# Start-up work moved between engines and rows, and the DMA queue in program order, in a fused window-attention and Fourier kernel

## The chip, the cores and the metric

The kernel runs on one core of one Trainium2 chip. The metric is the device time of one execution in microseconds (us), as the median of several runs. A second source is one profiled execution of the same program; its times come from the hardware profiler. Engine names in the profile: PE is TensorE (PEld its weight loads), DVE is VectorE, ACT is ScalarE, POOL is GpSimd, SP is the engine whose queue issues nearly all DMAs.

## What is computed

The input `x` holds 32 images of 56 x 56 pixels with 128 channels, in float32. Two layers follow each other, each with a residual:

```python
x = x + window_attention(group_norm(x))      # 7x7 windows, shifted by 3, 4 heads of 32
x = x + fourier_block(group_norm(x))         # 32 groups in both norms

# window_attention, for each of 64 windows of 49 pixels
q, k, v = split(win @ w_qkv.T);  q = q * hd ** -0.5
a = softmax(q @ k.T + bias + mask)           # bias from rpb_table, mask for the shifted edge
out = (a @ v) @ w_proj.T + b_proj

# fourier_block: along W with w0 and along H with w1
y = dct(x)[..., :32];  y = einsum("bixy,ioy->boxy", y, w);  y = idct(y padded to 56)
h = y_along_w + y_along_h
out = relu(h @ W1 + b1) @ W2 + b2            # 128 -> 512 -> 128
```

## The kernel before

**Rows and cycles.** The work is a software pipeline. An image has eight window rows (`NWR = 8`), and the main loop runs over cycles; cycle `r` is also called row `r`, counted from 0 over all images, so that row `8 * b + i` is window row `i` of image `b`. In cycle `r` the kernel computes q, k, scores and v of row `r` (`attn_qk`, `attn_scores`, `attn_v`), the softmax of rows around it (`attn_max` with a subtraction on GpSimd, `attn_exp` on ScalarE, `attn_divide` with a multiplication on GpSimd), the transposes of the probabilities of rows `r-1` and `r-2` (`attn_transpose`), the values of row `r-3` (`attn_values`) and its projection (`attn_project`), and the sums for the second norm (`attn_sums`) of row `r-4` or near it. Rows 0 to 10 go through `first_rows`, where nothing else runs.

**The Fourier part** of an image starts 11 cycles after its first row (`CONV_BEGIN = NWR + 3`). Its step `c = r - 11 - 8 * b` runs from 0 to 15: the transforms (`transform`) along W at c = 0 and along H at 1 and 2, the mixing (`mix`) at 3, 4 and 5, the transforms back (`modes_back`) at 5 to 8, and seven groups of feed-forward (`ff_in`, `ff_out`) at the steps of `FF_AT = (8, 9, 10, 12, 13, 14, 15)`. Two images are therefore in this part at once. Feed-forward first runs in row 19; later it is missing from one row in eight, where c is 3 for one image and 11 for the other (row 22, 30 and so on). What a step passes on goes through DRAM: `scr` (the residual stream), `zscr` (mixed modes). `load_columns` reads `htok` tiles from `scr`, `load_modes` reads `zT` tiles from `zscr`, `ff_in` reads `res` from `scr`, and `ff_out` writes `out_dram` from it.

**The next image.** Its load (`xl`, two buffers) is issued by `image_begin` at window row 3 of the image before, the second part at row 4. `image_groups(im, j)` turns rows `j` and `j+1` by seven TensorE transposes into two PSUM banks, copies them to `xw` on ScalarE (three copies), takes statistics on VectorE (L297) and adds the projection's bias into the image on GpSimd (`image_bias`, L306). Four such calls make an image. `image_norm` is a Python generator: each `next(norm)` emits one stage, namely the group statistics on VectorE with the power on GpSimd (`rstd`, L355); then `nb` on VectorE (L359) and the scaling of the weights on ScalarE (`wn`, L362); then a small matmul for the bias of v (L112, `pa<-nb,wqkv`) and its copy (`bqkv`, L367). `fourier_stats` does the same for the second norm (`tot`, L581, then two matmuls with `gmean`).

**PSUM and order.** There are eight PSUM banks, four for attention (`attn_bank`, `pa` in the profile) and four for the rest (`conv_bank`, `pc`). On PE, ACT, DVE and POOL the order of instructions is the order of the program, written out by hand:

```python
with tc.manual_schedule(engines={ET.PE, ET.Activation, ET.DVE, ET.Pool}):
```

On SP, the DMA queue, the scheduler chooses the order; an instruction of a queue that waits holds all that stand behind it. `bias_and_mask(0)` and `bias_and_mask(1)` add bias and mask into the constant `bm` for inner rows and for the last row of an image, 16 adds of 49 x 98 each on VectorE (L193); the second runs in row 1.

Of the kernel before, what the change touches and what calls it, by code (L numbers as in the profile page):

```python
# [15 lines left out]
P = 128  # L16
# [32 lines left out]
def swin_fourier_kernel(  # L49
# [33 lines left out]
    def attn_bank():  # L83
        return bank("pa", 4)
# [87 lines left out]
            )  # L172
    nc.sync.dma_start(rpb[JP : JP + WT], rpb[0:WT])

    mask_sb = work.tile([P, 4, C], F32, tag="sq", name="mask", bufs=1).rearrange("p n c -> p (n c)")
    mask_sb = mask_sb[:, : 4 * WT].rearrange("p (r k j) -> p r k j", r=2, k=2)
    nc.vector.memset(mask_sb, 0.0)
    for hh in range(2):
# [5 lines left out]
    nc.gpsimd.memset(bm, 0.0)  # L184
    rpb_f = rpb.rearrange("p (t u) y x -> p t u (y x)", u=2)

    def bias_and_mask(r):
        for t in range(2):
            for half in range(2):
                rows = slice(half * JP, half * JP + WT)  # L190
                for k, p0, p1 in ((0, 0, NP - half), (1, NP - half, NP)):
                    for p in range(p0, p1):
                        nc.vector.tensor_tensor(  # L193
                            bm[rows, r, t, p],
                            rpb_f[rows, t],
                            mask_sb[rows, r, k].unsqueeze(1).to_broadcast([WT, 2, WT]),
                            ALU.add,
                        )

    bias_and_mask(0)  # L200
    dct_w = const_load([TC, 2 * NM], dct, "dct_w")
    dct_h = const.tile([TC, 2 * NM], F32, tag="dct_h", name="dct_h")
    for r in range(0, TC, S):
# [63 lines left out]
    def image_groups(im, i):  # L267


        pt = [attn_bank(), attn_bank()]  # L270
        pts = [
            p[:, : n * S].rearrange("p (j r s) -> p j r s", r=n, s=WS) for p, n in zip(pt, (8, 6))
        ]
        for c in range(7):
            nc.tensor.transpose(  # L275
                pts[c // 4][:, :, 2 * (c % 4) : 2 * (c % 4) + 2],
                im.x[:, WS * i // 2 + c],
                ident_x[:, :, SS:].rearrange("p r (j s) -> p j r s", s=WS),
            )
# [35 lines left out]
    def image_norm(im):  # L315

        GR = C // 16

        def average(out, src):
            sums = small.tile([P, GR], F32, tag="gsums", name="gsums", bufs=2)  # L320
            nc.vector.tensor_reduce(
                sums, src.rearrange("p (g c) -> p g c", c=4), axis=AX.X, op=ALU.add
            )
            nc.vector.tensor_scalar(
                out.rearrange("p (g c) -> p g c", c=4),
                sums.unsqueeze(2).to_broadcast([P, GR, 4]),
                0.25,
                None,
                ALU.mult,
            )  # L330
# [24 lines left out]
        nc.gpsimd.tensor_tensor(rstd, ve, mhalf, ALU.pow)  # L355
        im.w = work.tile([P, 3 * C], F32, tag="wn", name="wn")
        yield
        nb = small.tile([P, 1], F32, tag="nb0", name="nb0")
        nc.vector.scalar_tensor_tensor(  # L359
            out=nb, in0=gm, scalar=-1.0, in1=rstd, op0=ALU.mult, op1=ALU.mult  # L360
        )
        nc.scalar.mul(im.w, wqkv, rstd)  # L362
        yield
        pb = attn_bank()
        halved(pb[:, 0:1], wqkv[:, 2 * C :], nb)
        im.bias = small.tile([P, 5], F32, tag="bqkv", name="bqkv")
        nc.vector.tensor_copy(im.bias[:, 2:3], pb[:, 0:1])  # L367
        yield

# [365 lines left out]

    def ff_in(im, g):
        t0, n = sum(FF_GROUPS[:g]), FF_GROUPS[g]
        k, last = n // P, n % P  # L740
        xff = im.xf.rearrange("p r w -> p (r w)")
        scr_tok = im.scr.rearrange("h w c -> (h w) c")
        res = work.tile([P, 4, C], F32, tag="res", name="res")
        nc.sync.dma_start(
# [1 line left out]
        )  # L746
        if last:
            nc.sync.dma_start(res[:last, k], scr_tok[t0 + k * P : t0 + n])
        for c0, c1, m in ((0, k, P), (k, k + 1, last)):
            if m:  # L750
                nc.gpsimd.tensor_tensor(  # L751
# [83 lines left out]
    def load_back(cycle):  # L835
        for im, c in fourier(cycle):
            for width, g in back_groups(c):
                load_modes(im, width, g)

    def nothing():  # L840
        while True:
            yield

    def load_first(cycle):
        for im, c in fourier(cycle):
# [3 lines left out]

    def halves_first(cycle, norm):  # L850
        for im, c in fourier(cycle):
            if c == 0:
                im.stats = fourier_stats(im)
                im.cols = {}
                next(im.stats)
        last, j = row(cycle - 4)
        sums = attn_sums(last, j) if last and cycle > CONV_BEGIN else nothing()
        next(sums)
        im, i = row(cycle)
        if im:  # L860
            attn_qk(im, i, False)
        next(norm)
        next(sums)
        for im, c in fourier(cycle):
            if c in FF_AT:
# [25 lines left out]
                    mix(im, True, g)  # L891

    def quarters(cycle):
        im, i = row(cycle)
        if im:
            attn_scores(im, i, cycle)
        for im, c in fourier(cycle):
            for width, g in back_groups(c):
                modes_back(im, width, g)

    def eighths(cycle):
        im, i = row(cycle - 3)
# [13 lines left out]
    def next_groups(cycle):  # L916
        b, i = divmod(cycle, NWR)
        if b + 1 < NB:
            for j in {(4 if b == 0 else 5): (0, 2), (5 if b == 0 else 6): (4, 6)}.get(i, ()):
                image_groups(images[b + 1], j)  # L920

    def last_out(cycle):
# [4 lines left out]
    def halves_last(cycle, norm):  # L927
# [6 lines left out]
        load_back(cycle + 1)  # L934
        next_begin(cycle)
        load_first(cycle)
        next(norm)
        if row(cycle)[0]:
            attn_exp(cycle)
            attn_divide(cycle)  # L940
# [1 line left out]
        if im:  # L942
            last_out(cycle)
            attn_project(im, j)
        next(norm)

    def next_begin(cycle):
        b, i = divmod(cycle, NWR)
# [7 lines left out]
    def first_rows(cycle, norm):  # L956
# [15 lines left out]
            attn_max(cycle)  # L972
        if im3:
            attn_project(im3, i3)
        next(norm)
        last, j = row(cycle - 4)
        if last:
            for _ in attn_sums(last, j):
# [2 lines left out]
            attn_v(im, i, cycle)  # L981
        if cycle < NWR // 2:
            image_bias(im, 2 * cycle)
        if cycle == 1:
            bias_and_mask(1)
        next(norm)
        next_begin(cycle)
        next_groups(cycle)
        if cycle == CONV_BEGIN - 1:
            attn_exp(cycle)  # L990
            attn_divide(cycle)
            for _ in attn_sums(im3, i3):
                pass
            last, j = row(cycle - 1)
            attn_transpose(last, j, cycle - 1)
        next(norm)

    ET = mybir.EngineType
    with tc.manual_schedule(engines={ET.PE, ET.Activation, ET.DVE, ET.Pool}):
        images[0] = image_begin(0)  # L1000
        for i in range(0, NWR, 2):
            image_groups(images[0], i)
        for _ in image_norm(images[0]):
            pass
        norm = nothing()
        for cycle in range(NB * NWR + CONV_BEGIN + FF_AT[-1] - NWR + 1):
            if cycle < CONV_BEGIN:
                first_rows(cycle, norm)
            else:
# [10 lines left out]
                    half_columns(cycle)  # L1020
                eighths(cycle)
                quarters(cycle)
                if row(cycle)[0] and cycle % 2:
                    attn_max(cycle)
                full(cycle)
                halves_last(cycle, norm)
            b, i = divmod(cycle, NWR)
            norm = nothing()
            if i == (NWR - 2 if b else NWR - 3) and b + 1 < NB:
                norm = image_norm(images[b + 1])  # L1030
                next(norm)


# [60 lines left out]
```

## Time and profile before

| | |
|---|---|
| median of 3 runs | 3635.16 us (3634.94 to 3637.57) |
| profiled execution | 3641.7 us, span 3639.9 us |
| mean granted TensorE clock | 0.995 of full speed |
| busy share PE, PEld, DVE, ACT, POOL | 98%, 78%, 61%, 59%, 38% |
| DMA | 390.31 MB, mean 107 GB/s |

The span is the time from the first to the last instruction of the profiled execution. A line of the profile names the source line, the engine, the operation, the tiles (written tile before the arrow) and the shape. In a timeline the first two numbers are start and duration in us, and a bracket gives the idle time before and the event that ended it; "issue" there means that the profile shows no event. In the list of waits the three numbers are the total, the count and the longest. Much of a helper's work has the line of the helper: L112 is `halved`, which issues most matmuls.

### The profile page before, as it was taken

The page shows a single profiled execution, that of the slowest core. Times are in us where ns is not written, and L with a number is a line of the kernel's source. Part 1 is how long each engine was busy: PE and PEld are TensorE (multiplying, and loading weights), DVE is VectorE, ACT ScalarE, POOL GpSimd, SP SyncE. Part 2 cuts the span into 40 slices and gives each one's busy share as a digit, 9 for nine tenths or more (in the row PEclk, how much of TensorE's full clock was granted, in tenths as well). Part 3 has the DMA queues.
Part 4 walks back from the last instruction along what each step waited for, and adds up shares of the span by engine and source line. Part 5 has one row for each costly group of instructions (what it writes and reads, how often), then busy time and mean ns, then how long its engine had stood idle before and what let it go on. Part 6 is the DMA issues. An engine that isn't in the chain of part 4 may idle for free.

```text
span 3639.9 us, 161666 instructions
## 1 busy us (share of the span) xinstructions
PE 3574.4 (98%) x72192; PEld 2832.6 (78%) x72192; DVE 2211.9 (61%) x4738; ACT 2148.1 (59%) x4044; POOL 1368.3 (38%) x1421
## 2 busy tenths in 40 slices
PE   7899999999999999999999999999999999999999
PEld 5677777778777787877777878777777777787776
DVE  7766666666666666666656656666566666565641
ACT  4555566655566555666556665556665556655553
POOL 5433333333343433333333434333333334343321
PEclk8999999999999999999999999999999999999999
DMA  4334434444434444334444344443444443444343
GB/s 114 86 102 112 113 96 111 108 110 111 112 97 112 112 109 116 94 110 107 113 108 111 94 114 109 113 114 94 111 108 111 110 111 94 114 109 109 97 115 98
DMA packets 687350, 390.31 MB, mean 107 GB/s; under 512 B 39967, under 2 KB 657600, under 8 KB 686400
## 3 DMA queue, kind: packets, MB, share of 16 engines
q1 hardware_dynamic: 686045, 379.65, 38.3%
q8 instruction: 568, 9.31, 1.1%
q14 instruction: 126, 1.03, 0.1%
q10 hardware_dynamic: 611, 0.32, 0.0%
HBM read 218.29 MB, written 161.48 MB: 104 GB/s over the span
## 4 chain that ended last, share of the span: by engine, by line
PE 92%; DVE 4%; issue 1%; ACT 1%; POOL 1%; DMA 1%; SPq 0%; POOLq 0%; DVEq 0%; ACTq 0%
PE pc L112 37%; PE pa L112 14%; PE pa L408 6%; PE pc L679 6%; PE pa L474 6%; PE pc L645 6%; PE pa L430 5%; PE pa L499 4%; PE pc L718 4%; PE pa L275 3%; DVE a L438 1%; DVE xf L729 0%; DVE oT L530 0%; POOL rstd L616 0%; ACT a L455 0%
## 5 line engine op out<-in xcount | busy, mean ns | idle before, releaser
L449 POOL TENSOR_TENSOR a<-a,mx 128x784 f32<-128x784 f32 x256 | 389.4, 1521 | 1427.3 <-DVE mx L448 1203.4
L112 PE MATMUL pc<-wff,hid 128*64 128x128 f32 x12544 | 740.3, 273 | 1.5 <-ACT hid L763 0.8
L112 PE MATMUL pc<-xf,wff 128*64 128x512 f32 (+2 forms) x3584 | 717.5, 539 | 1.1 <-DVE xf L729 1.0
L112 PEld LDWEIGHTS pc<-wff,hid 128*64 128x64 f32 x12544 | 702.6, 137 | 8.2 <-ACT hid L763 4.5
L460 DVE TENSOR_REDUCE sm<-a 128x16 f32<-128x784 f32 x256 | 248.2, 970 | 686.1 <-ACT a L455 682.8
L463 POOL TENSOR_TENSOR a<-a,rs 128x784 f32<-128x784 f32 x256 | 389.1, 1520 | 566.6 <-DVE rs L462 542.8
L763 ACT ACTIVATE hid<-pc,b1sb 128x512 f32<-128x512 f32 (+2 forms) x896 | 527.1, 632 | 76.6 <-PE pc L112 74.5
L112 PEld LDWEIGHTS pc<-xf,wff 128*64 128x64 f32 x3584 | 279.8, 137 | 368.0 <-issue 260.5
L379 ACT ACTIVATE q<-pa,bqkv 128x392 f32<-128x392 f32 x256 | 150.4, 587 | 473.1 <-PE pa L112 467.5
L112 PE MATMUL pa<-xw,wn 128*64 128x392 f32 (+1 forms) x2048 | 390.6, 497 | 3.7 <-DVE aT L484 2.7
L530 DVE TENSOR_SCALAR oT<-pa,bqkv 128x98 f32<-128x98 f32 (+2 forms) x768 | 171.0, 278 | 268.7 <-PE pa L499 268.6
L751 POOL TENSOR_TENSOR res<-res,b2sb 128x512 f32<-128x512 f32 (+2 forms) x256 | 264.2, 1037 | 113.5 <-DMA res<-scr 113.5
L408 PE MATMUL pa<-wn,xw 128*64 128x128 f32 x4096 | 283.6, 280 | 4.7 <-issue 3.5
L306 POOL TENSOR_TENSOR xl<-xl,bproj 112x512 f32<-112x512 f32 (+1 forms) x256 | 286.8, 1142 | 0.0
L499 PEld LDWEIGHTS pa<-aT,v 49*32 49x32 f32 x16384 | 172.9, 106 | 146.1 <-issue 127.0
L415 ACT COPY v<-pa 128x512 f32<-128x512 f32 x256 | 150.9, 589 | 228.3 <-PE pa L408 228.3
L438 DVE TENSOR_TENSOR a<-pa,bm 128x392 f32<-128x392 f32 x512 | 264.8, 559 | 25.8 <-PE pa L430 2.1
L455 ACT ACTIVATE a<-a 128x784 f32<-128x784 f32 x256 | 222.3, 869 | 97.2 <-POOL a L449 96.8
L482 ACT COPY aT<-pa 113x452 f32<-113x452 f32 x256 | 139.4, 544 | 210.4 <-PE pa L474 206.6
L408 PEld LDWEIGHTS pa<-wn,xw 128*64 128x64 f32 x4096 | 221.4, 137 | 38.6 <-issue 9.1
L112 PE MATMUL pa<-wproj,oT 128*64 128x128 f32 (+1 forms) x3584 | 248.0, 274 | 1.8 <-DVE oT L530 1.8
L448 DVE TENSOR_REDUCE mx<-a 128x16 f32<-128x784 f32 x256 | 246.3, 962 | 4.3
(91 smaller groups left out, 5583.8 us busy)
## 6 DMA issues: line engine op xcount, KB each, us to landing
zscr<-z SPq DMA_DIRECT2D x512, 112.0 KB
htok<-scr SPq DMA_DIRECT2D x256, 196.0 KB
zT<-zscr SPq DMA_DIRECT2D x192, 256.0 KB
res<-scr SPq DMA_DIRECT2D x160, 256.0 KB
out_dram<-res SPq DMA_DIRECT2D x160, 256.0 KB
scr<-xl SPq DMA_DIRECT2D x128, 224.0 KB
xl<-in_x_dram SPq DMA_DIRECT2D x32, 784.0 KB
xl<-in_x_dram SPq DMA_DIRECT2D x32, 672.0 KB
```

The costliest lines, as they stand in the source:

```text
L112: nc.tensor.matmul(dst[ps], lhsT=lhsT[:, ps], rhs=rhs, start=start, stop=stop)
L306: nc.gpsimd.tensor_tensor(piece, piece, bproj.unsqueeze(1).to_broadcast([TC, e - a, C]), ALU.add)
L408: nc.tensor.matmul(pv[hs, j * C : (j + 1) * C], lhsT=im.xw[i][:, w * WT : w * WT + JP], rhs=im.w[:, 2 * C : 3 * C], start=True, stop=True,)
L438: nc.vector.tensor_tensor(a[:, 2 * hp : 2 * hp + 2, :, 0:WT].rearrange("p u w j -> p w u j"), ps[hp][:, :RT].rearrange("p (w u j) -> p w u ...
L448: nc.vector.tensor_reduce(mx, a3, axis=AX.X, op=ALU.max)
L449: nc.gpsimd.tensor_tensor(a3, a3, mx.unsqueeze(2).to_broadcast([P, 2 * NWR, WT]), ALU.subtract)
L455: nc.scalar.activation(a3, a3, AF.Exp)
L460: nc.vector.tensor_reduce(sm, a3, axis=AX.X, op=ALU.add)
L463: nc.gpsimd.tensor_tensor(a3, a3, rs.unsqueeze(2).to_broadcast([P, 2 * NWR, WT]), ALU.mult)
L499: nc.tensor.matmul(po4[u][h * HD : (h + 1) * HD, 2 * f + e], lhsT=v[ks, 2 * f + e, h * HD : (h + 1) * HD], rhs=im.aT[i][f][ks, h, e * JP : ...
L751: nc.gpsimd.tensor_tensor(res[:m, c0:c1], res[:m, c0:c1], b2sb[:m].unsqueeze(1).to_broadcast([m, c1 - c0, C]), ALU.add,)
L763: nc.scalar.activation(hf[:, :n], ph[:, :n], AF.Relu, bias=b1sb[:, f : f + 1])
```

## The change

- `image_groups` takes its two banks from the attention banks or, for every second call, from the other four. From image 2 on, all four calls stand in window row 6 of the image before; formerly two in row 5 and two in row 6. For image 1 they stay in rows 4 and 5.
- `bias_and_mask` takes an engine. The half for the last window row moves from VectorE in row 1 to GpSimd in rows 4 and 5, eight adds each. The mask is kept in a `res` buffer until then.
- The three stages of `image_norm` move apart: statistics in the same row as before, scaling in the next call, and the small matmul in the row after, behind q and k of the image's first row. For image 0 it comes after the scores of row 0.
- For image 0's second norm, `fourier_stats` starts in row 10, ahead of `attn_exp` and `attn_divide`, with `attn_sums` of row 7 ahead of them too.
- In rows without feed-forward, `modes_back` stands ahead of `attn_scores`.
- SP joins the engines in program order, and the load of `res` is issued one row earlier (`load_residual` from `load_back(cycle + 1)`).

```diff
-    mask_sb = work.tile([P, 4, C], F32, tag="sq", name="mask", bufs=1).rearrange("p n c -> p (n c)")
+    mask_sb = work.tile([P, 4, C], F32, tag="res", name="mask").rearrange("p n c -> p (n c)")
...
-    def bias_and_mask(r):
-        for t in range(2):
-            for half in range(2):
...
+    def bias_and_mask(engine, r, t, half):
+        rows = slice(half * JP, half * JP + WT)
+        for k, p0, p1 in ((0, 0, NP - half), (1, NP - half, NP)):
+            for p in range(p0, p1):
+                engine.tensor_tensor(
...
-    bias_and_mask(0)
+    for t in range(2):
+        for half in range(2):
+            bias_and_mask(nc.vector, 0, t, half)
...
-        pt = [attn_bank(), attn_bank()]
+        pt = [conv_bank() if i % 4 else attn_bank() for _ in range(2)]
...
+    def load_residual(im, g):
+        t0, n = sum(FF_GROUPS[:g]), FF_GROUPS[g]
+        k, last = n // P, n % P
+        scr_tok = im.scr.rearrange("h w c -> (h w) c")
+        res = work.tile([P, 4, C], F32, tag="res", name="res")
+        nc.sync.dma_start(
+            res[:, :k], scr_tok[t0 : t0 + k * P].rearrange("(n p) c -> p n c", p=P)
+        )
+        if last:
+            nc.sync.dma_start(res[:last, k], scr_tok[t0 + k * P : t0 + n])
+        im.next_res = res
...
     def ff_in(im, g):
-        res = work.tile([P, 4, C], F32, tag="res", name="res")
-        nc.sync.dma_start(
...
+        res = im.next_res
...
     def load_back(cycle):
...
+            if c in FF_AT:
+                load_residual(im, FF_AT.index(c))
...
+    def start_stats(im):
+        im.stats = fourier_stats(im)
+        im.cols = {}
+        next(im.stats)
...
     def halves_first(cycle, norm):
         for im, c in fourier(cycle):
-            if c == 0:
-                im.stats = fourier_stats(im)
-                im.cols = {}
-                next(im.stats)
+            if c == 0 and cycle > CONV_BEGIN:
+                start_stats(im)
...
-        next(norm)
+        if has_ff(cycle):
+            next(norm, None)
...
     def quarters(cycle):
+        def back():
+            for im, c in fourier(cycle):
+                for width, g in back_groups(c):
+                    modes_back(im, width, g)
+        if not has_ff(cycle):
+            back()
         im, i = row(cycle)
         if im:
             attn_scores(im, i, cycle)
-        for im, c in fourier(cycle):
-            for width, g in back_groups(c):
-                modes_back(im, width, g)
+        if has_ff(cycle):
+            back()
...
-            for j in {(4 if b == 0 else 5): (0, 2), (5 if b == 0 else 6): (4, 6)}.get(i, ()):
+            for j in ({4: (0, 2), 5: (4, 6)} if b == 0 else {6: (0, 2, 4, 6)}).get(i, ()):
                 image_groups(images[b + 1], j)
...
     def first_rows(cycle, norm):
...
-        if cycle == 1:
-            bias_and_mask(1)
-        next(norm)
+        if cycle in (4, 5):
+            for half in range(2):
+                bias_and_mask(nc.gpsimd, 1, cycle - 4, half)
...
         if cycle == CONV_BEGIN - 1:
+            start_stats(im3)
+            for _ in attn_sums(im3, i3):
+                pass
             attn_exp(cycle)
             attn_divide(cycle)
-            for _ in attn_sums(im3, i3):
-                pass
...
-    with tc.manual_schedule(engines={ET.PE, ET.Activation, ET.DVE, ET.Pool}):
+    with tc.manual_schedule(engines={ET.PE, ET.Activation, ET.DVE, ET.Pool, ET.SP}):
...
-        for _ in image_norm(images[0]):
-            pass
-        norm = nothing()
+        norm = image_norm(images[0])
+        for _ in range(3):
+            next(norm)
...
+                if not has_ff(cycle):
+                    next(norm, None)
                 if row(cycle)[0] and cycle % 2:
                     attn_max(cycle)
```

More of the change, by code (lines that the diff above doesn't have):

```diff
@@ L185, in swin_fourier_kernel @@
     rpb_f = rpb.rearrange("p (t u) y x -> p t u (y x)", u=2)
-    def bias_and_mask(r):
-        for t in range(2):
-            for half in range(2):
[L190 to L198, printed above, removed]
-    bias_and_mask(0)
+    def bias_and_mask(engine, r, t, half):
[3 more added lines that the diff above has]
+                engine.tensor_tensor(
+                    bm[rows, r, t, p],
+                    rpb_f[rows, t],
+                    mask_sb[rows, r, k].unsqueeze(1).to_broadcast([WT, 2, WT]),
+                    ALU.add,
+                )
+    for t in range(2):
+        for half in range(2):
+            bias_and_mask(nc.vector, 0, t, half)
     dct_w = const_load([TC, 2 * NM], dct, "dct_w")
@@ L356, in image_norm @@
         im.w = work.tile([P, 3 * C], F32, tag="wn", name="wn")
+        im.bias = small.tile([P, 5], F32, tag="bqkv", name="bqkv")
         yield
@@ L365, in image_norm @@
         halved(pb[:, 0:1], wqkv[:, 2 * C :], nb)
-        im.bias = small.tile([P, 5], F32, tag="bqkv", name="bqkv")
         nc.vector.tensor_copy(im.bias[:, 2:3], pb[:, 0:1])
@@ L734, in modes_back @@
                 nc.scalar.copy(dst[:, li], src.rearrange("p (c h r) -> p c h r", c=nch, r=2))
-    def ff_in(im, g):
+    def load_residual(im, g):
         t0, n = sum(FF_GROUPS[:g]), FF_GROUPS[g]
         k, last = n // P, n % P
-        xff = im.xf.rearrange("p r w -> p (r w)")
         scr_tok = im.scr.rearrange("h w c -> (h w) c")
@@ L748, in ff_in @@
             nc.sync.dma_start(res[:last, k], scr_tok[t0 + k * P : t0 + n])
+        im.next_res = res
+    def ff_in(im, g):
+        t0, n = sum(FF_GROUPS[:g]), FF_GROUPS[g]
+        k, last = n // P, n % P
+        xff = im.xf.rearrange("p r w -> p (r w)")
+        res = im.next_res
         for c0, c1, m in ((0, k, P), (k, k + 1, last)):
@@ L944, in halves_last @@
             attn_project(im, j)
-        next(norm)
     def next_begin(cycle):
@@ L974, in first_rows @@
             attn_project(im3, i3)
-        next(norm)
+        next(norm, None)
         last, j = row(cycle - 4)
@@ L983, in first_rows @@
             image_bias(im, 2 * cycle)
-        if cycle == 1:
-            bias_and_mask(1)
-        next(norm)
+        if cycle in (4, 5):
+            for half in range(2):
+                bias_and_mask(nc.gpsimd, 1, cycle - 4, half)
         next_begin(cycle)
@@ L989, in first_rows @@
         if cycle == CONV_BEGIN - 1:
+            start_stats(im3)
+            for _ in attn_sums(im3, i3):
+                pass
             attn_exp(cycle)
             attn_divide(cycle)
-            for _ in attn_sums(im3, i3):
-                pass
             last, j = row(cycle - 1)
             attn_transpose(last, j, cycle - 1)
-        next(norm)
     ET = mybir.EngineType
-    with tc.manual_schedule(engines={ET.PE, ET.Activation, ET.DVE, ET.Pool}):
+    with tc.manual_schedule(engines={ET.PE, ET.Activation, ET.DVE, ET.Pool, ET.SP}):
         images[0] = image_begin(0)
@@ L1022, in swin_fourier_kernel @@
                 quarters(cycle)
+                if not has_ff(cycle):
+                    next(norm, None)
                 if row(cycle)[0] and cycle % 2:
@@ L1027, in swin_fourier_kernel @@
             b, i = divmod(cycle, NWR)
-            norm = nothing()
             if i == (NWR - 2 if b else NWR - 3) and b + 1 < NB:
                 norm = image_norm(images[b + 1])
-                next(norm)
+                next(norm, None)
 def _constants():
```

## The prediction

> **What bounds the kernel now.** I read the page's shares and slices first. PE's digits, with the granted clock:
>
> ```profile
> PE 3574.4 (98%) x72192; PEld 2832.6 (78%) x72192; DVE 2211.9 (61%) x4738; ACT 2148.1 (59%) x4044; POOL 1368.3 (38%) x1421
> PE   7899999999999999999999999999999999999999
> PEclk8999999999999999999999999999999999999999
> ```
>
> TensorE is full except at the start. The windows by slice (window, PE, PEld, DVE, ACT, POOL, clock, DMA) give sizes:
>
> ```profile
> 0.00:91.00 91.00, 64.60 (x1032) 46.82 (x1032) 64.90 (x163) 44.77 (x93) 47.48 (x62) 0.89 0.45 114
> 91.00:182.00 91.00, 77.35 (x1734) 63.37 (x1732) 65.46 (x142) 53.58 (x106) 38.91 (x39) 0.94 0.32 86
> 182.00:273.00 91.00, 86.58 (x1760) 68.44 (x1762) 58.98 (x129) 51.02 (x96) 36.22 (x39) 0.98 0.37 102
> 2729.90:2820.90 91.00, 90.81 (x1850) 71.73 (x1850) 57.14 (x118) 54.34 (x102) 35.17 (x39) 1.00 0.42 111
> ```
>
> Idle: 44.5 us in the first three slices, 15 in the 36 that follow, 6 in the last. So steady rows (row = cycle, numbered from 0) can only lose, and the last slice is one image's TensorE work. All gain lies before row 19, where feed-forward fills TensorE. The waits of TensorE name what to look for, its timeline where:
>
> ```profile
> PE pa L112 <- DVE nb L359: 10.3, 3, 4.7
> PE pa L112 <- DVE tot L581: 4.0, 1, 4.0
> 77.12 0.38 PE L112 MATMUL pa<-nb,wqkv 128*64 128x1 f32 x4 [4.41 <-DVE nb L359]
> 113.39 0.34 PE L112 MATMUL pa<-tot,gmean 112*64 112x64 f32 x4 [3.97 <-DVE tot L581]
> 128.01 0.57 PE L499 MATMUL pa<-aT,v 49*32 49x49 f32 x29 [2.08 <-issue]
> ```
>
> Then the timelines of VectorE, GpSimd and the DMA queue where these idle times are:
>
> ```profile
> 33.69 6.23 DVE L193 TENSOR_TENSOR bm<-rpb,mask 49x98 f32<-49x98 f32 x16
> 40.61 0.97 DVE L460 TENSOR_REDUCE sm<-a 128x16 f32<-128x784 f32 x1
> 84.52 1.04 DVE L438 TENSOR_TENSOR a<-pa,bm 128x392 f32<-128x392 f32 x2 [0.48 <-PE pa L430]
> 56.48 1.52 POOL L449 TENSOR_TENSOR a<-a,mx 128x784 f32<-128x784 f32 x1 [0.44 <-DVE mx L448]
> 63.24 1.52 POOL L463 TENSOR_TENSOR a<-a,rs 128x784 f32<-128x784 f32 x1 [0.67 <-DVE a L438]
> 71.05 1.52 POOL L463 TENSOR_TENSOR a<-a,rs 128x784 f32<-128x784 f32 x1 [0.17 <-DVE rs L462]
> 110.39 1.78 SPq L667 DMA_DIRECT2D htok<-scr  x4
> 118.77 4.53 SPq L118 DMA_DIRECT2D xl<-in_x_dram  x5
> ```
>
> VectorE is busy 4.6 to 4.9 of every 5 us from 55 to 75; GpSimd in rows 4 and 5 waits 0.7 and 0.2 us only. Below, times are on the clock of before.
>
> **A. Mask off VectorE at row 1.** The 16 adds hold 33.69 to 39.92. The next sum (L460) starts at 40.61; without them its input binds, the exponent of row 1, 35.52 + 0.87 = 36.4 in ScalarE's timeline. Gain 4.2. The 2.68 us that TensorE idles before 40.63 go too, and with them slow matmuls (clock 0.70 and 0.62 from 40 to 50: eight transposes 1.86 us against 1.39 later): 0.8, bounds 0 and 1.6 (five slow groups). Sum -5.0 (-3.4, the sum delayed by other VectorE work, to -5.8).
>
> **B. Mask on GpSimd in rows 4 and 5, norm over three rows.** The bias matmul that waited 4.41 us moves behind row 8's q and k, nb and the weight scaling to row 7. (The first of the three nb waits, 4.7 us at 18.07 before row 0, stays for another reason: q needs the scaled weights, down at 17.77 + 0.61, and its matmul already started at 18.43. Zero.) What is late next is GpSimd. No row shows a 49x98 add on it. L751's 1277 ns for 512 columns and 730 for 256 give 2.14 ns a column, hence 392 ns at 98; bounds 185 (VectorE's first eight, 1.48 us undisturbed) and 448 (its 64x128 add). I take 392, from its own rows: eight cost 3.1 us. GpSimd then runs: subtraction of row 4 to 58.0, mask 61.1, image adds (57.94 to 62.57 before, 4.6) 65.7, multiply 67.2, subtraction of row 5 68.7, mask 71.8, adds 76.4, multiply 77.9, subtraction of row 6 79.4. Row 6's transposes (68.10) and exponent (68.67) are still met; row 7's transposes wait 2.7 us. Exponent 0.87, sum 0.97 and reciprocal 0.25 put row 7's scores add at 81.5 instead of 84.52: -3.0. The step to row 8's took 7.5 us with half-rate matmuls, the next 6.7: -0.8. Sum -3.8; with 185 ns VectorE's own queue binds at 79.6, -5.7; with 448, -2.0 without the second part.
>
> The same adds took 6.23 / 16 = 0.39 us on VectorE beside a busy GpSimd, so the move costs nothing in length. [...]
>
> An idle time near 2.7 us remains. In this trace 2.08 us was followed by clocks of 0.73 and 0.58, 2.68 us by 0.70 and 0.62, 1.79 us by 1.00; I therefore count no clock recovery there beyond the 0.8. [...]
>
> **C. Statistics ahead of the exponent, row 10.** L581 now follows row 7's residual add: mx ends 107.12, two sums 108.6, tot 109.2, two sums of row 7 110.4; matmuls at 110.5, not 113.39, -3.0. The 112 transforms behind ran 4.96 us where later ones take 3.45. VectorE's scores add of row 11 follows at 116.1, not 120.31; ScalarE's exponent at 119.9, not 124.08. Sum -4.2 (-3.0 where only the idle time goes, -5.5 where all 3.97 of it and 1.5 of slow transforms go).
>
> **D. SP in program order.** In row 11 the four column loads (htok, 196 KB each) now stand behind the first piece of image 2's load (784 KB), which waits for the last transform of image 0 at T = 118.63, since it takes its buffer. The tail shows the rate: 256 KB issued at 3615.37 let GpSimd start at 3618.19, 768 KB issued from 3587.66 at 3592.39, so 1.9 us per further 512 KB. Columns land at T + 6.4 and T + 7.8; wanted T + 4.5. Transforms end at T + 8.7, not T + 6.2, but before lost 0.37 + 2.08 just behind and ran slow: scores ended at T + 11.4, now T + 10.4. Sum -1.0 (-2.5 if the load is quicker, +3 if the 2.08 us, whose releaser is not shown, comes again on top). Later images have 13 us between transform and columns for 6.3 us of transfer: zero. Each row's zT loads now wait for the z copies (378.59 + 0.58, row 23), with 1.2 MB queued: down by about 385, wanted 388.91; zero, cover 4 us.
>
> **E. Transposes in one block.** Row 14 (image 2) has four groups. ScalarE copies a group in 0.9 us, TensorE transposes one in 0.8 to 0.95: from the aT copy's end near 151.5 the twelve copies take 3.7, then v to 155.8, z to 156.7 and 157.6 at TensorE's pace, and only then the exponent, before at 156.28. GpSimd's 9.4 us of adds end by 162.5, its multiply by 164.0, before row 15's subtraction is due (166.10). +1.2 (0 to +2.5). From image 3 on (row 22 and every eighth) no feed-forward stands in this row. Covers: the third group's banks are free at 365.18 (VectorE's second aT copy), wanted 365.7; GpSimd ends its adds at 375.7 and the multiply at 377.2, while the norm's rstd is due at 377.3. Zero; its price if cover fails is a rival.
>
> **F. Transforms back ahead of scores.** It applies only without feed-forward: rows 16, 17, 18. Scores waited for k on VectorE (0.39, 1.90, 1.70 us); the work now stands in these waits. Row 16: values end 171.05, transforms 172.9, scores 173.8, a 174.8, aT copy 175.4, where mx starts, not 175.78; row 17: VectorE binds, 0; row 18: the four xf adds (1.75) move ahead of a, mx at 195.5, not 196.56. Sum -1.4 (+1.5 if the adds wait, -2).
>
> **G. Residual a row ahead**: GpSimd's 113.5 us of waiting for it are off the chain: zero. Its issue (0.38 us on SP) moves past out_dram and scr and, in an image's row 3, past the image and column loads; none of those is late by that. The mask's other buffer and bqkv's earlier tile: zero.
>
> Sum: -5.0 - 3.8 - 4.2 - 1.0 + 1.2 - 1.4 = -14.2. The profiled execution, 3641.7 (span 3639.9 and 1.8 around it), becomes 3627.5; it lies 6.5 above the median 3635.16, which becomes **3621.0**. Ends: -21.5 all good, -1.1 all bad.
>
> **Rivals.** *Block stalls in every image*: if the four groups' copies, image adds or the SP order hold TensorE in the FF-free row, it costs 30 times. Slower by 0.2% (7.3 us, about what a measurement can tell) needs (14.2 + 7.3) / 30 = 0.72 us each; 1.65 us, the two added groups unhidden, gives 3621 + 50 = 3671. For it: the 0.5 us cover of the banks; against: 15 us idle in 36 slices says these rows have had no queue trouble. 0.11.
> *Eaten start*: GpSimd's mask at VectorE's worst (four in 3.07 us) and the column stall in full: -14.2 + 3.8 + 4 = -6.4, 3629. For it: GpSimd's short waits in rows 4 and 5. 0.14.
> *Clock*: mean clocks 0.89, 0.94, 0.98 hold 17 us over three slices; with the gaps shorter, more than I count comes back, -20 or more, 3614. 0.09.
>
> **Numbers.** Forecast case (gain 7.3 to 20) 0.66. Faster 0.75 with the clock case, same 0.14, slower 0.11. Range 3614 to 3631: below lies part of the clock case, above the stall and half of the eaten start.
>
> **What would show it.** Right: no L193 on VectorE after 26 us, none of the nb or tot waits; row 7's transposes wait about 3 us for GpSimd's multiply; a wait for htok near 115; slices 4 to 39 idle as before. Wrong: new idle of TensorE every 112 us in the row with 28 transposes; waits for zT or htok past 220 us; first-three-slice idle still above 38 us.

## The result and the profile after

| | before | after |
|---|---|---|
| median | 3636.36 us (3634.94 to 3638.27, 4 runs) | 3615.95 us (3613.83 to 3618.46, 4 runs) |
| profiled execution | 3641.7 us, span 3639.9 | 3618.46 us, span 3616.7 |

The ratio is 0.9944, 95% interval 0.9927 to 0.9961: 20.4 us faster, where 14.2 was forecast and 3614 to 3631 was the range. The time is inside the range; most of the reasons were not. Where the time went shows in a ledger: the interval between the first scores matmul of one row and that of a later row (the starts of L430, in after L431, read from the trace). Like every ledger below, it is of the one profiled execution of each kernel.

| rows | before | after | difference | forecast |
|---|---|---|---|---|
| 0 to 28 (all the start-up) | 310.1 us | 307.5 us | -2.5 | -14.2 |
| 28 to 255 (steady) | 3153.3 us | 3131.5 us | -21.8 | 0 |

Ahead of row 0 after is 0.4 us longer and behind row 255 0.8 us, so the two spans differ by 23.2 us.

The page of after looks like that of before; TensorE does the same 72192 matmuls in 17 us less busy time:

```profile
PE 3557.3 (98%) x72192; PEld 2829.6 (78%) x72192; DVE 2254.9 (62%) x4722; ACT 2145.9 (59%) x4044; POOL 1376.0 (38%) x1437
PE   7899999999999999999999999999999999999999
```

The windows by slice (columns as in the prediction) say the same from the other side: the first three slices idle 26.3, 12.5 and 3.9 us, 42.7 together where before had 44.5. The prediction had named more than 38 there as a sign that it was wrong. The 36 slices behind them idle 9.8 us where before had 14.9.

```profile
0.00:91.00 91.00, 64.69 (x1054) 47.02 (x1056) 64.60 (x146) 45.32 (x94) 52.84 (x78) 0.89 0.42 108
91.00:182.00 91.00, 78.51 (x1788) 63.71 (x1782) 65.43 (x143) 53.69 (x106) 39.19 (x39) 0.94 0.35 88
182.00:273.00 91.00, 87.08 (x1714) 67.80 (x1708) 59.84 (x127) 51.88 (x99) 36.38 (x38) 0.98 0.43 106
```

In TensorE's list of waits nb (10.3 us) and tot (4.0 us) are gone, and three others stand there (total, count, longest; the 5.1 of wn is the start of row 0, its other 3.3 is in row 16):

```profile
PE pa L112 <- ACT wn L364: 8.3, 2, 5.1
...
PE pa L475 <- POOL a L464: 3.4, 1, 3.4
PE pc L646 <- DMA htok<-scr: 3.4, 2, 3.0
```

**The steady gain is in the transposes of the next image.** TensorE's timeline in before, one steady image: two blocks of 14, each from its first start to the start of what follows 1.65 and 1.91 us, 3.56 in all:

```profile
681.28 1.72 PE L275 MATMUL pa<-ident_x,xl 112*128 112x112 f32 x14
682.93 1.09 PE L408 MATMUL pa<-wn,xw 128*64 128x128 f32 x16
...
696.06 1.98 PE L275 MATMUL pa<-ident_x,xl 112*128 112x112 f32 x14
697.97 1.09 PE L408 MATMUL pa<-wn,xw 128*64 128x128 f32 x16
```

In after the 28 stand in one block, 691.88 to 694.86, 2.98 us:

```profile
691.88 0.92 PE L276 MATMUL pa<-ident_x,xl 112*128 112x112 f32 x7
692.64 0.88 PE L276 MATMUL pc<-ident_x,xl 112*128 112x112 f32 x7
693.35 0.88 PE L276 MATMUL pa<-ident_x,xl 112*128 112x112 f32 x7
694.06 0.87 PE L276 MATMUL pc<-ident_x,xl 112*128 112x112 f32 x7
694.86 1.09 PE L409 MATMUL pa<-wn,xw 128*64 128x128 f32 x16
```

Over images 4 to 29 the means are 3.56 and 2.99. Idle time makes only 0.04 us of the difference. One transpose is recorded with 262 ns while the next starts 100 ns after it, so a wait of up to some 160 ns lies inside the recorded duration and is counted as busy. The starts of the single records tell: a step is 0.1016 us on average, 28 make 2.84; the first step of a block takes 0.05 more and the last 0.09 more (0.145 a block); and in the second block of before the 11th step takes 0.30 and the one behind it 0.157. TensorE goes on at 697.52, just when VectorE ends a copy that frees a bank:

```profile
696.85 0.62 DVE L484 COPY aT<-pa 113x452 f32<-113x452 f32 x1
```

So before pays two block entries (0.29) and 0.43 of waits for banks, after one entry (0.145) and none. 0.576 us for each of the 28 images turned between rows 28 and 255 is 16.1 of the 21.8 us. Of the other 5.7 some 4 are TensorE's idle time outside these blocks, 13.1 us in before's execution and 9.1 in after's, most of it in waits for which the profile shows no event; the remaining 1.6 us are spread over many groups, and their cause is open. Idle time between rows 28 and 255 varies between executions (7.3 to 14.2 us in all the profiles here, before's is the longest), and before's profiled execution is 5.3 us above its median where after's is 2.5 above its own.

**The start-up** gained in three places and gave most of it back. VectorE's and GpSimd's timelines in row 6 of after:

```profile
73.33 3.48 DVE L325 TENSOR_SCALAR gmeans<-gsums 128x32 f32<-128x32 f32 x1
76.84 1.45 DVE L340 TENSOR_TENSOR turned<-turned,gmeans 128x32 f32<-128x32 f32 x1
...
81.51 0.96 DVE L461 TENSOR_REDUCE sm<-a 128x16 f32<-128x784 f32 x1
...
82.74 0.97 DVE L439 TENSOR_TENSOR a<-pa,bm 128x392 f32<-128x392 f32 x2
```

```profile
73.08 2.21 POOL L307 TENSOR_TENSOR xl<-xl,bproj 112x512 f32<-112x512 f32 x2
75.25 1.52 POOL L464 TENSOR_TENSOR a<-a,rs 128x784 f32<-128x784 f32 x1
76.72 1.52 POOL L450 TENSOR_TENSOR a<-a,mx 128x784 f32<-128x784 f32 x1
```

The same two operations in before's row 6:

```profile
74.24 0.25 DVE L324 TENSOR_SCALAR gmeans<-gsums 128x32 f32<-128x32 f32 x1
74.53 0.19 DVE L339 TENSOR_TENSOR turned<-turned,gmeans 128x32 f32<-128x32 f32 x1
```

Operations that take 0.18 and 0.19 us where GpSimd rests took 3.48 and 1.45, and each ended 0.04 to 0.05 us behind a GpSimd operation (76.81 and 76.77; 78.29 and 78.24). So VectorE was late for the sum of row 7 (L461): its input, the exponent, was ready at 79.14 in ScalarE's timeline, and it began at 81.51, 2.4 us later; the scores add of row 7 (L439) stands right behind it. TensorE's timeline has what followed, with the columns and row 16's scaled weights:

```profile
76.82 1.86 PE L475 MATMUL pa<-ident,a 113*113 113x113 f32 x8 [3.41 <-POOL a L464]
...
122.95 1.04 PE L646 MATMUL pc<-dct_h,htok 112*64 112x64 f32 x28 [3.05 <-DMA htok<-scr]
...
164.72 2.64 PE L112 MATMUL pa<-xw,wn 128*64 128x393 f32 x8 [3.26 <-ACT wn L364]
```

### The profile page after: what moved, and what is told of

Read it like the earlier page. It is cut to its first block, busy times and chain, and to the rows that moved or that the text cites. A ratio compares the mean times of both kernels' runs of the same rounds, so it can differ in the third digit from the quotient of the medians.

```text
span 3616.7 us, 161664 instructions
## 1 busy us (share of the span) xinstructions
PE 3557.3 (98%) x72192; PEld 2829.6 (78%) x72192; DVE 2254.9 (62%) x4722; ACT 2145.9 (59%) x4044; POOL 1376.0 (38%) x1437
## 4 chain that ended last, share of the span: by engine, by line
PE 93%; DVE 4%; ACT 1%; POOL 1%; DMA 1%; issue 1%; SPq 0%; POOLq 0%; DVEq 0%; ACTq 0%
PE pc L112 38%; PE pa L112 15%; PE pa L409 6%; PE pc L680 6%; PE pa L475 6%; PE pc L646 6%; PE pa L431 5%; PE pa L500 4%; PE pc L719 4%; PE pa L276 1%; PE pc L276 1%; DVE a L439 1%; DVE xf L730 0%; DVE oT L531 0%; POOL rstd L617 0%
## 5 line engine op out<-in xcount | busy, mean ns | idle before, releaser
L461 DVE TENSOR_REDUCE sm<-a 128x16 f32<-128x784 f32 x256 | 248.2, 970 | 671.8 <-ACT a L456 668.5
L464 POOL TENSOR_TENSOR a<-a,rs 128x784 f32<-128x784 f32 x256 | 389.2, 1520 | 612.0 <-DVE rs L463 532.7
L307 POOL TENSOR_TENSOR xl<-xl,bproj 112x512 f32<-112x512 f32 (+1 forms) x256 | 287.3, 1145 | 0.2
L439 DVE TENSOR_TENSOR a<-pa,bm 128x392 f32<-128x392 f32 x512 | 264.9, 560 | 26.9 <-PE pa L431 2.9
L794 DVE TENSOR_TENSOR res<-pc,res 128x512 f32<-128x512 f32 (+3 forms) x257 | 138.6, 550 | 177.2 <-PE pc L112 134.6
```

The source lines that it names most:

```text
L307: nc.gpsimd.tensor_tensor(piece, piece, bproj.unsqueeze(1).to_broadcast([TC, e - a, C]), ALU.add)
L439: nc.vector.tensor_tensor(a[:, 2 * hp : 2 * hp + 2, :, 0:WT].rearrange("p u w j -> p w u j"), ps[hp][:, :RT].rearrange("p (w u j) -> p w u ...
L461: nc.vector.tensor_reduce(sm, a3, axis=AX.X, op=ALU.add)
L464: nc.gpsimd.tensor_tensor(a3, a3, rs.unsqueeze(2).to_broadcast([P, 2 * NWR, WT]), ALU.mult)
```

## The experiments

Each kernel ran beside runs of before on the same chip; differences are medians against that before, ratios with their 95% interval. Two theories of the steady gain: **T1**, the transposes; **T2**, the DMA queue's order with the earlier residual. Then the start-up's three losses, one by one.

### Part E alone, its halves, and after without it

Block and banks on before:

```diff
-        pt = [attn_bank(), attn_bank()]
+        pt = [conv_bank() if i % 4 else attn_bank() for _ in range(2)]
-            for j in {(4 if b == 0 else 5): (0, 2), (5 if b == 0 else 6): (4, 6)}.get(i, ()):
+            for j in ({4: (0, 2), 5: (4, 6)} if b == 0 else {6: (0, 2, 4, 6)}).get(i, ()):
```

> The kernel before with part E alone: the four groups of an image's transposes in one block in window row 6 (from image 2 on), their banks alternating between the two sets; nothing else is changed. Theory T1, the gain is in the transposes: in the trace of before an image's 28 transposes take 3.56 us from the first start to the start of what follows, in the trace of after 2.99; 30 images make 17 us, so this kernel takes 3617 to 3621 us and its 28 transposes 2.9 to 3.1 us an image. Theory T2, the gain is in the DMA queue's program order and the residual loaded a row ahead (less waiting and less contention in steady rows): this kernel is within 4 us of before, 3636. The prediction on record counted E at nothing in steady rows and +1.2 us in row 14: 3637.

3621.24 us, -15.1; 0.996 (0.9947 to 0.9972); transposes 2.99 us an image.

The first pair of lines alone:

> The kernel before with one line changed: every second group of transposes takes its two PSUM banks from the other set; the groups stay two and two in window rows 5 and 6. T1: the waits for banks inside the transposes go (about 0.42 us of the 0.58 us an image: a step of 300 ns where 100 is usual, and the slow first step after each), the second entry and exit of a block (0.15 us) stay, so 3.1 us an image and 3622 to 3626 us in all. T2: 3636.

3623.41 us, -12.9; 0.9969 (0.9957 to 0.9981); 3.14 us an image. Both blocks are now free of waits, 1.58 and 1.56 us long:

```profile
678.23 0.93 PE L275 MATMUL pa<-ident_x,xl 112*128 112x112 f32 x7
679.00 0.87 PE L275 MATMUL pc<-ident_x,xl 112*128 112x112 f32 x7
679.81 1.09 PE L408 MATMUL pa<-wn,xw 128*64 128x128 f32 x16
```

The second pair of lines alone:

> The kernel before with the four groups in one block in window row 6, but all eight banks from the attention set of four. T1: one entry and exit less saves 0.15 us an image, but the third and fourth group now wait for ScalarE's copies of the first and second (about 0.9 us a group against 0.72 us of transposes), so 3.3 to 3.9 us an image: 3628 to 3646 us, no clear gain. If the block and not the banks carried the gain: about 3620. T2: 3636.

3634.65 us, -1.7; 0.9996 (0.9987 to 1.0005); 3.34 us an image:

```profile
696.14 3.41 PE L275 MATMUL pa<-ident_x,xl 112*128 112x112 f32 x28
699.48 1.09 PE L408 MATMUL pa<-wn,xw 128*64 128x128 f32 x16
```

I had expected the third and fourth group to wait for ScalarE, and they did not: the single starts show 0.30 at the 11th step, as in before, and none behind it. That makes 2.84 + 0.145 + 0.35.

After with both pairs undone:

> The kernel after with part E alone undone (groups two and two in window rows 5 and 6, all from the attention banks); the DMA queue in program order, the residual a row ahead and all start-up parts stay. T1: the start-up's 2 us remain and 17 us come back: 3632 to 3636 us, 3.5 us of transposes an image. T2: 3616 to 3619, as after.

3629.1 us, -7.2; 0.998 (0.9971 to 0.9989); 3.57 us an image.

After without E came out 3 us below the range that T1 had given it. T1 holds all the same: the four transpose times close the account (2.84 + 2 x 0.145 + 0.43 = 3.56; without the waits 3.13; without one entry and the row-5 waits of 0.08, 3.34; without both 2.99), the medians follow them in order, and after without E falls back. The banks are worth 0.43 us an image, 30 x 0.43 = 12.9, and the median shows just that. The second entry, 0.145 us an image, shows in the length of the blocks only: the block alone should have gained 30 x 0.23 = 6.8 and gained 1.7 (interval a gain of 4.7 to a loss of 1.8), the block on top of the banks 2.2 of 4.4. Where the rest went was not found. After is 13 us faster than the kernel without E. What is left for all other parts is 7.2 us (4.0 to 10.5), half of the 15.4 forecast for them.

### The DMA queue's order alone

```diff
-    with tc.manual_schedule(engines={ET.PE, ET.Activation, ET.DVE, ET.Pool}):
+    with tc.manual_schedule(engines={ET.PE, ET.Activation, ET.DVE, ET.Pool, ET.SP}):
```

with `load_residual` from `load_back`, on before.

> The kernel before with part D and G alone: SP in program order and the residual loaded a row ahead. First theory (the prediction's D): steady rows gain nothing, their period stays at 111.3 us an image and the 28 transposes at 3.56 us; in row 11 the column loads stand behind the next image's load, TensorE waits 3 us for htok as in after (3.05 and 0.32 us), net 0 to +3 us: 3636 to 3639. Rival: the 7.2 us by which the kernel with only the groups undone beat before are the queue's order and not the start-up parts: 3629 to 3631.

3635.39 us, +0.9; 0.9998 (0.9989 to 1.0007). T2 falls: transposes 3.57 us an image, no gain in the median. (Its rows 28 to 255 take 3145.5 us against 3153.3, but before's profiled execution lies 5.3 us above its median and this one's at its own.) Row 11 is slower as in after:

```profile
126.96 3.20 PE L645 MATMUL pc<-dct_h,htok 112*64 112x64 f32 x56 [4.49 <-DMA htok<-scr]
```

Rows 11 to 12 take 12.25 us instead of 9.14, rows 12 to 15 30.21 instead of 31.92: D costs +1.4. Against the kernel with the banks alone, which also has the old order and whose rows 11 to 12 take 8.52 and rows 12 to 15 30.78, it costs 3.2. SP's queue in after has the new order; the columns, in before issued from 110.39 on, stand behind the load that waits for the transforms of row 11, over at 113.86:

```profile
114.01 0.32 SPq L118 DMA_DIRECT2D xl<-in_x_dram  x1
114.38 3.43 SPq L668 DMA_DIRECT2D htok<-scr  x4
```

### Columns first, mask elsewhere, norm elsewhere, on after

```diff
-        next_begin(cycle)
         load_first(cycle)
+        next_begin(cycle)
```

> The kernel after with the column loads (htok) issued ahead of the next image's load in the same row. If row 11's wait of 3.05 us for htok and the slow clock behind it (0.91 and 0.50) cost what they show: the wait goes, row 12 starts its scores 2 to 4 us earlier, 3612 to 3614 us. Rival: another limit takes its place before feed-forward starts (VectorE, or the transforms' own buffers): htok's wait gone, but feed-forward starts within 1 us of after, 3615 to 3617. Steady rows: no difference under either.

3615.5 us, -19.0; 0.9943 (0.993 to 0.9955). The wait is gone (rows 11 to 12 8.53 us instead of 12.37, rows 0 to 28 300.8 instead of 307.5), yet the median did not move: rows 28 to 255 take 3137.2 us instead of 3131.5.

```diff
-        if cycle in (4, 5):
-            for half in range(2):
-                bias_and_mask(nc.gpsimd, 1, cycle - 4, half)
+        for t, half in {1: ((0, 0),), 3: ((0, 1), (1, 0)), 6: ((1, 1),)}.get(cycle, ()):
+            bias_and_mask(nc.gpsimd, 1, t, half)
```

> The kernel after with GpSimd's 16 mask adds in rows 1, 3 and 6 (4, 8, 4) instead of 8 each in rows 4 and 5. Theory: with no queue behind them on GpSimd the norm's small operations on VectorE take 0.2 us again (in after one took 3.48 and one 1.45, each ending with a GpSimd operation), row 7's transposes do not wait 3.41 us for GpSimd's multiplication, VectorE's scores add of row 7 starts at 77.5 to 79.5 instead of 82.74, 3612 to 3614 us in all. Rival: the slow VectorE operations have nothing to do with GpSimd's queue, stay, and the time is that of after, 3616.

3607.91 us, -26.6; 0.9921 (0.9908 to 0.9935): the same adds on the same engine, in rows where its queue has room. VectorE's two operations:

```profile
70.29 0.65 DVE L325 TENSOR_SCALAR gmeans<-gsums 128x32 f32<-128x32 f32 x1
70.97 0.19 DVE L340 TENSOR_TENSOR turned<-turned,gmeans 128x32 f32<-128x32 f32 x1
```

Row 7's transposes do not wait, its scores add starts at 75.6 instead of 82.74, and row 6 to 7 takes 7.12 us instead of 11.03. Rows 4 to 8 together take 32.82 us instead of 37.80. The edit removes GpSimd's late multiplication and VectorE's late norm at once; by the trace of after VectorE's lateness for the sum (2.4 us) is about half of these 5.0, an estimate, and no run separates the two. With the adds spread VectorE's own queue sets the pace: the exponent of this sum is ready at 72.19, and the sum starts at 74.38 behind other VectorE work. VectorE's 0.65 us again ends 0.04 us behind a GpSimd operation (70.94 and 70.90).

```diff
-        norm = image_norm(images[0])
-        for _ in range(3):
-            next(norm)
+        for _ in image_norm(images[0]):
+            pass
+        norm = nothing()
```

> The kernel after with image 0's bias matmul (nb) back ahead of row 0, all three stages of its norm before the first row, as in before. Theory: in after it takes a fifth attention bank between row 0's scores and v, so that q of row 1 must wait for the bank of the scores (2.18 us for VectorE's add); ahead of row 0 that wait is gone and row 1's scores start at 28.9 to 29.9 instead of 30.97. 3614.5 to 3616 us, since rows 4 to 6 are bound by VectorE. Rival: the bank is late for the scores add itself, which waits for the bias tables, and the wait moves to k: 30.5 to 31, 3616.

3612.91 us, -21.6; 0.9935 (0.9923 to 0.9948), not distinguishable from after. Row 1's scores started at 30.85: the wait for the bank was gone, but the q and k matmuls of row 1 ran 2.81 us instead of 2.02, so my theory of row 1 found no support.

The norm's stage back to `halves_first` in rows 15 and 16 (`next(norm, None)` in every row, the one behind `quarters` removed):

> The kernel after with the norm's stage of rows 15 and 16 (image 2; the only rows it touches) back behind q and k, where before had it, instead of behind the transforms and the scores. Theory: the step from row 15's scores to row 16's grew from 11.03 us (before) to 13.07 (after, and 13.06 in the kernel with the groups undone) because the scaled weights come 3.26 us too late for row 16's q; with the stage back it is 10.5 to 11.8, row 16's wait for wn gone, 3613.5 to 3615 us in all. Rival: the statistics then delay row 15's scores add on VectorE, and the steps before or after take the 2 us back: 3616.

3620.72 us, -18.2; 0.9947 (0.9934 to 0.9959). The rival was right: wn's wait went, oT's took its place, and row 15 to 16 is 13.69 us, not shorter.

```profile
162.00 0.86 PE L112 MATMUL pa<-wproj,oT 128*64 128x128 f32 x12 [3.33 <-DVE oT L531]
```

Here too one of the norm's operations (0.19 us elsewhere) stands beside a GpSimd multiplication that ends at 159.36:

```profile
157.96 1.45 DVE L340 TENSOR_TENSOR turned<-turned,gmeans 128x32 f32<-128x32 f32 x1
```

### Towards a version that beats both

> The kernel after with the mask adds spread over rows 1, 3 and 6 and the column loads ahead of the next image's load. If both gains stand (row 6 to 7 in 7.1 us instead of 11.0, row 11 to 12 in 8.5 instead of 12.4, of which rows 12 to 15 give 0 to 1.5 back): 3604 to 3607 us. Rival: the earlier columns find their limit in VectorE, or the image loads behind them hold up a steady row, and the time is that of the mask alone, 3608, or above.

3617.54 us, -21.4; 0.9937 (0.9925 to 0.995).

> The kernel after with all three: mask adds in rows 1, 3 and 6, column loads first, image 2's norm behind q and k. If the three add up: 3602 to 3605 us. Rival: the norm's move only shifts the wait, and the time is within 1 us of the kernel with the first two.

3617.97 us, -20.9; 0.9938 (0.9925 to 0.9952).

Both missed their forecasts and came out behind the mask alone although rows 0 to 28 were about as long (297.2 and 300.0 us against its 299.6). Rows 28 to 255 took 3137.3 and 3138.9 us, as with the columns first alone; the four other kernels with part E of after, so far, 3129.3 to 3134.8.

```diff
+        if cycle == CONV_BEGIN:
+            load_first(cycle)
         next_begin(cycle)
-        load_first(cycle)
+        if cycle > CONV_BEGIN:
+            load_first(cycle)
```

> The kernel after with the mask adds in rows 1, 3 and 6, and the column loads ahead of the image load in row 11 alone; later images keep the order of after. Theory: the three kernels with the columns first everywhere spent 6 us more between rows 28 and 255 (3137 to 3139 us) than the mask kernel (3129), which is the order's doing; without it in steady rows that stretch is 3129 to 3132 again, and row 11's gain (4 us, of which row 14 gives 1.6 back) stays: 28 to 30 us below the before of its own call. Rival: the 6 us are chance or come from what row 11 sets off, the stretch is 3135 or more, 21 to 25 us below before.

3608.8 us, -29.6; 0.9917 (0.9903 to 0.993). Rows 28 to 255 are back at 3130.8 us, row 11 to 12 at 8.51. So the order of the loads seems to cost steady rows time in three kernels out of three, 7 to 8 us beside the two other kernels on one chip, 2.5 to 4 beside the one on another (the norm in rows 15 and 16 moved back, 3134.8). TensorE's idle time there is 12.9 to 14.2 us where the five others have 7.3 to 12.2, mostly in waits for which the profile shows no event; why is open. This kernel beats before and, in the median, after; against the mask spread alone (0.9921) its interval overlaps.

## Why the prediction was right and wrong

The number held by luck, because an error of one sign covered another: all parts but E gave 7.2 us (4.0 to 10.5) instead of 15.4, and E gave 13 to 15 in steady rows instead of nothing there and a cost of 1.2 in row 14. The ledger by stretch, in us between scores:

| rows | before | queue alone | after without E | after | mask spread | columns in row 11 too |
|---|---|---|---|---|---|---|
| 0 to 4 | 29.91 | 28.85 | 25.93 | 28.74 | 25.94 | 28.10 |
| 4 to 7 | 30.02 | 30.28 | 27.45 | 27.46 | 23.56 | 23.56 |
| 7 to 8 | 7.77 | 7.80 | 9.36 | 10.34 | 9.26 | 8.21 |
| 8 to 11 | 28.70 | 28.71 | 24.73 | 24.73 | 24.72 | 24.43 |
| 11 to 12 | 9.14 | 12.25 | 12.49 | 12.37 | 13.00 | 8.51 |
| 12 to 15 | 31.92 | 30.21 | 30.20 | 31.91 | 30.98 | 33.76 |
| 15 to 16 | 11.03 | 11.50 | 13.06 | 13.07 | 13.08 | 13.05 |
| 16 to 19 | 34.09 | 33.84 | 31.70 | 31.84 | 31.85 | 31.99 |
| 28 to 255 | 3153.3 | 3145.5 | 3146.5 | 3131.5 | 3129.3 | 3130.8 |

- **What bounds the kernel: wrong here.** "Steady rows can only lose" was read from 15 us of idle in 36 slices. The idle column misses waits that are shorter than what a pipelined matmul's record covers (262 ns where the next starts after 100); the 0.43 us an image were visible only in the length of the two blocks. Both profiles show the steady slices as full, and one does the same matmuls in 17 us less. This step failed, and with it **E** ("zero" in steady rows). My 0.5 us cover of the banks named the very copy (VectorE's aT) that in before did hold the second block, but was only asked of after. In row 14 E was to cost 1.2; after lost 0.8 there (12.29 to 13.07), E alone 2.3, and another 1.4 in row 15 to 16 (12.46).
- **A, -5.0: too much.** The sum of row 1 was released as forecast (row 2 to 3 takes 5.34 us instead of 10.51, which is -5.2), but row 0 to 1 grew from 5.92 to 7.64 and row 3 to 4 from 7.51 to 9.06, so rows 0 to 4 gave 1.2 in this execution and 4.0 in after without E, whose start-up differs by E alone. Between those two lies the clock, see below. No undoing of A alone was run.
- **B, -3.8: the step that failed is VectorE's side.** GpSimd's length was right (eight adds 2.68 and 2.95 us, forecast 3.1), and so was row 7's wait (3.41, forecast 2.7). One add took 0.34 to 0.37 us on GpSimd in after; on VectorE in before it took 0.39 in row 1, where GpSimd was busy for part of the time, and 0.185 while GpSimd was idle (1.48 for eight). So the move cost nothing in length against the 0.39 only. But I priced VectorE's norm as if GpSimd's later queue did not touch it: from row 4's scores to row 7's scores add the forecast has 28.6 us (52.88 to 81.5), after took 30.7 (52.07 to 82.74), and the 2.4 us by which VectorE was late for the sum are about the difference. Row 4 to 7 gave 2.6, row 7 to 8 cost 2.6 instead of giving 0.8: B is worth nothing as built (rows 4 to 8 37.79 and 37.80 us). With the adds spread, rows 4 to 7 give 6.5 and row 7 to 8 costs 1.5, 5.0 together.
- **C, -4.2: right.** Row 10 to 11 takes 11.37 us instead of 15.70, -4.3, in each kernel that has it, and 15.71 to 15.77 in the four experiments that lack it. It was not run by itself.
- **D, -1.0: wrong sign, within its ends.** +3.1 in row 11, -1.7 behind it. The wait came (3.05 and 0.32), but the transfer was priced too short: with T, the end of the transforms, at 113.86 TensorE goes on with the columns at T + 9.1 and T + 10.4 (122.95 and 124.31), where the prediction had T + 6.4 and T + 7.8 from two loads at the kernel's end. Zero in steady rows held in the median of the queue's order alone.
- **F, -1.4: half.** Rows 16 to 19 gave 2.3. Row 15 to 16 took 2.0 more, which I did not count; there the scaled weights come 3.26 us late, since the norm's stage now stands behind the transforms. That this move is the cause is not shown: putting it back gained nothing. F was not run by itself.
- **G, zero**: not run apart from D; together they measured +0.9 us, not distinguishable from zero.
- **Rivals.** *Block stalls in every image* had the right place and the wrong sign. *Eaten start* (-6.4) met the start-up's size, by another mechanism than four slow adds. *Clock*: the trace's clock records put 34.1 us of half rate ahead of feed-forward in before and 34.1 in after, in pieces of 3.4, 6.8 and 10.2, so nothing came back in these two executions. But of four kernels whose start-up is that of after but for one detail, after without E had 13.7 us of half rate, the early norm 17.1, the norm in rows 15 and 16 moved back 23.9 and after 34.1, and rows 0 to 28 took 302.5, 303.3, 306.5 and 307.5 us. The half-rate time does differ, then, between executions of nearly the same start-up, and the start-up's length with it; after's profiled one was a long one. How much of this is chance and how much the one detail was not separated.

## What to carry over

A full engine can still hide waits: compare the length of the same group of instructions, first start to the next group's start, with its count times its usual step, before calling a stretch free of gain. When two engines' work is moved past each other, ask not only whose queue becomes longer but which small operations of the other engine now run beside it; the same sixteen adds were worth 5.0 us more (rows 4 to 8) in rows where GpSimd's queue had room. A forecast total that is met proves no step of it; a ledger by rows, over several kernels with parts taken out, does.

## What was not expected of the hardware

- Two small VectorE operations on SBUF in row 6 of after lasted until GpSimd's running operations were over: 3.48 us (L325) and 1.45 (L340) instead of 0.18 and 0.19; L340 again in the kernel with the norm back (1.45). The first lasted through three GpSimd instructions in a row (L307 twice, L464). Not every one does: the reduction just ahead of it (L322, 0.19) ran beside the same L307, and VectorE's adds with one input from PSUM took 0.97 for two of 128x392 beside GpSimd (L439 at 61.79 in after, L307 running from 60.11 to 64.64), no more than the 1.04 with GpSimd idle (L438 at 25.98 in before). L340 has two SBUF inputs, L325 and L322 have one; what sets the slow ones apart no run here shows.
- A separate block of transposes (112*128 in the profile's lines) ahead of matmuls of 128*64 took 0.145 us beyond its steps, 0.05 on entering and 0.09 on leaving, and each wait for a bank a slow step of 0.157 instead of 0.10 behind it. The leaving step took 0.19 instead of 0.10 in every block ahead of these matmuls; the block of transposed probabilities is alike, its last step takes 0.19 ahead of the same matmuls and 0.10 ahead of these transposes. Why these steps are longer was not shown.
- The place of a 0.8 MB load in the DMA queue, four column loads earlier or later, went with 2.5 to 8 us in 227 steady rows without any wait that names it, in one profiled execution of each kernel.
